# Convolution on raw padded rows: the second normalization moved from the data into the tap weights, and the last image split into quarters

## The chip, the core and the metric

One core of a Trainium2 chip runs the whole kernel. The metric is the device time of one execution in microseconds. Three runs of the kernel before took 4033.33, 4034.28 and 4036.42 us; the median is 4034.28.

Five engines work on their own queues, in the order in which the program issues to each: PE (TensorE, with its weight loads PEld), DVE (VectorE), ACT (ScalarE), POOL (GpSimd) and SP (SyncE, which here only issues DMAs).

## The reference, cut to what matters

The input x has 16 images of 56 x 56 positions with 384 channels, in float32. Both layers add a residual to a group normalization over 32 groups of 12 channels.

```
x = x + L0_conv(gn(x))      # window attention: 7x7 windows of the image rolled by 3, 12 heads of 32,
                            # w_qkv (1152x384), w_out (384x384), b_out, relative position bias and masks
x = x + L1_conv(gn(x))      # depthwise 3x3 convolution, zero padding, one sign (+1, 0, -1) per tap and channel
```

`gn(v) = (v - mean) / sqrt(var + 1e-5)`, per image and group of channels. With a scale a and a shift s per channel and image it is a*v + s. The zero padding stands around the normalized image, so that at the image's border fewer than nine taps see the shift s.

## The kernel before, in words

Channels lie on the 128 partitions, in NC = 3 blocks. An image is NS = 8 strips of 7 rows (a row of windows), a strip is two units of 4 windows; so there are NU = 16 units per image and 256 units, numbered u = 0 to 255. `all_units` (L1014) issues them one by one. The heavy work of a unit is on PE: `value`, `query_key` and `project` (three matmuls of 392 columns per output block), `scores` of the next unit, `add_up` and `attend` of this one. DVE adds the bias to the scores (`softmax`, L587, the operation e), takes part in the reciprocal (`invert`, L681 and L682), scales (`divide`, L689), turns values (`turn`, L527), and adds the residual (`project`, L708) with statistics (L714). ACT empties PSUM, takes exponentials (L605) and logarithms (L679, L680). `by_key` (L534) moves the turned values with 16 DMAs on SP, for which `add_up` of the next strip waits. PSUM has four banks for products (`bank`) and four for scores.

Beside this runs light work, at due times: `at(when, f, ...)` puts a function into the list of the unit int(when), at the fraction after the point. `plan_load` (L964) brings in the next image: `fetch_halves` issues on POOL (L450) the input DMAs of a strip two strips ahead, 12 for a strip of whole rows and 48 for the strip that wraps around the rolled image, which is the last of the eight. `plan_conv` (L946) does the second layer of the image before. `norm_gather` and `norm_scale` bring the statistics to POOL by DMA and compute a and s there; `center` (L731) derives the middle tap's coefficients. Then come six chunks, half an image (28 rows) and one channel block each, `step` units apart (2.6, for the last but one image 1.95), after a lead of 3 units:

- `band` (L742), SP: loads 30 rows of the strip sums, which `project` had written to the DRAM tile `mid`, into `xb`, of which there is one.
- `pad` (L777), ACT, L792: writes a*x + s into one of two zero-bordered tiles `hp`.
- `middle` (L808), ACT, L822: starts the sum `o` with the residual and the middle tap.
- `tap` (L824), DVE, L828: eight operations o = hp * w + o over 1568 elements.
- `turn_sum` (L832), DVE, L835, and `store` (L837), SP: turns the sum to tokens and writes it in eight DMAs.

The last image has no next one to hide behind. `plan_last` (L908) puts its statistics (`norm_products` with matmuls, L340), four chunks of the first two channel blocks on DVE, and the third channel block in four quarters on PE after the last unit: `convolve` (L849) adds 8 taps and the middle as nine matmuls for each of 28 pieces of 112 tokens (L865, L872), `carry` (L874) and `turn_late` (L888) write out. The bands are loaded in two parts, since the last strip, which holds the rows 52 to 55 and 0 to 2, is complete only at the end. At the very end a check value is computed (L1102 to L1111) and read by all engines; a second, safer program is skipped.

Of the kernel before, what the change touches and what calls it, by code (L numbers as in the profile page):

```python
# [34 lines left out]
def kernel(  # L35
# [30 lines left out]
    R = W + SHIFT  # L66
    LT = 2 * W
# [17 lines left out]
    bpool = ctx.enter_context(tc.tile_pool(name="xb", bufs=1))  # L85
# [23 lines left out]
    dw_t = const.tile([P, NC, 9], F32, tag="dw", name="dw_t")  # L109
    bias = const.tile([P, 2, NH, 2, T], F32, tag="bias", name="bias")  # L110
# [13 lines left out]
    hps = [const.tile([P, BR + 2, W + 2], F32, tag=f"hp{n}", name=f"hp{n}") for n in range(2)]  # L124

    accs = [const.tile([P, 2 * BR, D], F32, tag=f"o{n}", name=f"o{n}") for n in range(2)]
# [22 lines left out]
    def clear_conv():  # L149
        for t in (*xls, *hps, *accs):  # L150
            nc.gpsimd.memset(t, 0.0)
# [42 lines left out]
    def load_depthwise():  # L194
# [10 lines left out]
        nc.vector.tensor_copy(dw_t, pw[:, : NC * 9].rearrange("p (c t) -> p c t", c=NC))  # L205

    loaded_bias = []

    def load_bias(queue, first_q, last_q, fast):


        if not loaded_bias:
            rel = ypool.tile([P, NC, WIN, R], F32, tag="y", name="rel").rearrange("q c h w -> q (c h w)")[:, : T * NH]
            nc.gpsimd.memset(rel, 0.0)
            loaded_bias.append(rel)
# [15 lines left out]
        mask = ypool.tile([P, NC, WIN, R], F32, tag="y", name="mask").rearrange("q c h w -> q (c h w)")[:, : 2 * T]  # L231
# [80 lines left out]
    def fetch_late():  # L312
# [3 lines left out]
        def place(name, rows, width, at=None):  # L316
# [7 lines left out]
        hp = [  # L324
            place("hp_late", LR + 2, W + 2, xls[1].rearrange("p t c -> p (t c)")),
            place("hp_late2", LR + 2, W + 2),
        ]
        acc = [
            place("acc_late", LR, W + 2, xt.rearrange("p c k d -> p (c k d)")),
            place("acc_late2", LR, W + 2),  # L330
        ]
        for t in (*hp, *acc):
            nc.gpsimd.memset(t, 0.0)
        late_tiles.update(gm=gm, dg=dg, hp=hp, acc=acc)
# [5 lines left out]
    def norm_products(key, gm, meanwhile=()):  # L340
        st = stats.pop(key)
# [24 lines left out]
        for f, n in meanwhile[:1]:  # L366
            f(n)
# [7 lines left out]
        for f, n in meanwhile[1:]:  # L375
            f(n)
# [10 lines left out]
    def late_norm(b):  # L387
        norm_products((1, b), late_tiles["gm"])

    xs = {}  # L390
# [5 lines left out]
    def fetch(s):  # L396
        b, r = divmod(s, NS)
        xl = staging(s)
        first = r * WIN + SHIFT
# [38 lines left out]
    def fetch_halves(s, c):  # L438
# [6 lines left out]
        first = r * WIN + SHIFT  # L445
# [133 lines left out]
    def softmax(u, fast):  # L579
# [4 lines left out]
        if fast:  # L584
# [6 lines left out]
            bias[:, int(s % NS == NS - 1)].rearrange("q (i j) w k -> q i (j w) k", i=HPC),  # L591
# [99 lines left out]
    def project(s, m):  # L691
# [4 lines left out]
        if m == 0:  # L696
            ys[s] = ypool.tile([P, NC, WIN, R], F32, tag="y", name=f"y_{s}")
# [9 lines left out]
        view = ys[s][:, m, :, SHIFT:R]  # L707
# [7 lines left out]
        if m == NC - 1:  # L715
            if b not in mids:
                mids[b] = dram.tile([P, NC, H, R], F32, tag="mid", name=f"mid_{b}")
            del xs[s]
            yt = ys.pop(s)
            nc.gpsimd.tensor_copy(yt[:, :, :, 0:SHIFT], yt[:, :, :, W:R])  # L720
            r0 = r * WIN + SHIFT
            n = min(WIN, H - r0)
            queue = nc.sync if s == B * NS - 1 else nc.gpsimd
            queue.dma_start(mids[b][:, :, r0 : r0 + n, :], yt[:, :, 0:n, :])
            if n < WIN:
                queue.dma_start(mids[b][:, :, 0 : WIN - n, :], yt[:, :, n:WIN, :])
# [4 lines left out]
    def center(b, pool=nc.gpsimd):  # L731

        coef = coefs[1, b]
        cen = small.tile([P, NC, 2], F32, tag="cen", name=f"cen_{b}")
        pool.tensor_tensor(cen[:, :, 0], coef[:, :, 0], bo_sb, ALU.mult)
        pool.tensor_tensor(coef[:, :, 1], coef[:, :, 1], cen[:, :, 0], ALU.add)
        pool.tensor_tensor(cen, coef, dw_t[:, :, 4].unsqueeze(2).to_broadcast([P, NC, 2]), ALU.mult)
        pool.tensor_scalar(cen[:, :, 0], cen[:, :, 0], 1.0, None, ALU.add)
        pool.tensor_tensor(cen[:, :, 1], cen[:, :, 1], bo_sb, ALU.add)
        centers[b] = cen  # L740

    def band(b, k, c):  # L742
# [3 lines left out]
        xb = bpool.tile([P, BR + 2, R], F32, tag="xb", name=f"xb_{b}_{k}_{c}")  # L746
        nc.sync.dma_start(xb[:, at : at + hi - lo, :], mids[b][:, c, lo:hi, :])
        bands[b, k, c] = (xb, at, hi - lo)

    last_strip = ((0, (NS * WIN + SHIFT) % H), ((NS - 1) * WIN + SHIFT, H))  # L750

    def band_late(b, k, c, part):

        rows = LR if c == NC - 1 else BR
        lo, hi = max(k * rows - 1, 0), min((k + 1) * rows + 1, H)
        first = k * rows - 1
        if part == 0:
            size = (rows + 2) * R
            if c == NC - 1:
                xb = xpool.tile([P, NC, ST], F32, tag="x", name=f"xb_late_{k}").rearrange("p c n -> p (c n)")  # L760
            elif (k, c) == (0, 1):
                xb = qk.rearrange("p m n -> p (m n)")
            elif (k, c) == (1, 0):
                xb = bias.rearrange("p v h w n -> p (v h w n)")
            else:
                xb = bpool.tile([P, BR + 2, R], F32, tag="xb", name=f"xb_{b}_{k}_{c}").rearrange("p h w -> p (h w)")
            bands[b, k, c] = (xb[:, :size].rearrange("p (h w) -> p h w", w=R), lo - first, hi - lo)
        xb = bands[b, k, c][0]
        parts = [(last_strip[0][1], last_strip[1][0])] if part == 0 else last_strip
        for p0, p1 in parts:  # L770
            p0, p1 = max(p0, lo), min(p1, hi)
            if p0 < p1:
                nc.sync.dma_start(xb[:, p0 - first : p1 - first, :], mids[b][:, c, p0:p1, :])

    count, padded = [0], {}

    def pad(b, k, c, late=False):  # L777

        coef = coefs[1, b]
        xb, at, n = bands.pop((b, k, c))  # L780
        rows = LR if late else BR
        if late:
            hp = late_tiles["hp"][k % 2]
        else:
            hp = hps[count[0] % 2]
            outs[b, k, c] = accs[count[0] % 2]
            count[0] += 1
        if k == 0:
            nc.gpsimd.memset(hp[:, 0, :], 0.0)
        if k == H // rows - 1:  # L790
            nc.gpsimd.memset(hp[:, rows + 1, :], 0.0)
        nc.scalar.activation(  # L792
            hp[:, at : at + n, 1 : W + 1],
            xb[:, at : at + n, 0:W],
            AF.Identity,
            bias=coef[:, c, 1:2],
            scale=coef[:, c, 0:1],
        )
        padded[b, k, c] = (hp, xb)
# [8 lines left out]
    def middle(b, k, c, late=False, first=False):  # L808

        xb = padded[b, k, c][1]  # L810
        cen = centers[b][:, c]
        if late:
            acc = late_tiles["acc"][k % 2]
            outs[b, k, c] = acc
            to, rows = acc[:, :, :W], xb[:, 1 : LR + 1, 0:W]
        else:
            to, rows = sum_of(b, k, c), by_half(xb[:, 1 : BR + 1, 0:W])
# [244 lines left out]
    with tc.manual_schedule():  # L1062
# [11 lines left out]
        for n, home in ((0, hps[1]), (1, accs[0])):  # L1074
            fetch_weights(n, home)
# [100 lines left out]
```

## Time and profile before

| What | us |
|---|---|
| median of the three runs | 4034.28 |
| the profiled execution's own time | 4037.27 |
| its span | 4035.5 |
| PE busy | 3951.8 (98%) |
| DVE busy | 3493.2 (87%) |
| ACT busy | 2227.1 (55%) |
| POOL busy | 1867.7 (46%) |
| taps, L828, 752 operations on DVE | 1378.1, 1833 ns each |
| last softmax addition (unit 255) | starts at 3925.15 |
| last output DMA issued | 4028.60 |

The own time is the whole execution, and the span runs from the first to the last instruction. Busy time is summed per engine; engines overlap. A line of a group has the line in the code, the engine, the operation, what it writes and reads, its shape and its count, then the busy time and the mean of one in ns, then the engine's idle time ahead of it and what ended most of it. In a line in order of time the start comes first and then the duration, both in us. Starts of two operations of one engine that follow each other are a little closer than a duration, since an operation overlaps the next.

### The profile page before, as it was taken

How to read it: one execution, taken by the hardware profiler on the slowest of the kernel's cores; microseconds unless marked ns; L12 is line 12 of the kernel's file. 1: busy time of each engine (PE TensorE's matmuls, PEld its weight loads, DVE VectorE, ACT ScalarE, POOL GpSimd, SP SyncE). 2: the span in 40 equal slices, each digit the busy share in tenths (PEclk: the TensorE clock that was granted, in tenths of full speed). 3: DMA queues.
4: the chain of work that ended last, by engine and by line, in shares of the span. 5: the costliest groups of instructions: out<-in, count | busy, mean ns of one | idle time of the engine just before them, and what ended most of it. 6: DMA issues, size and time to landing. Idle time of an engine off the chain costs nothing.

```text
span 4035.5 us, 144674 instructions
## 1 busy us (share of the span) xinstructions
PE 3951.8 (98%) x63189; PEld 2415.2 (60%) x63189; DVE 3493.2 (87%) x3718; ACT 2227.1 (55%) x4690; POOL 1867.7 (46%) x3159
## 2 busy tenths in 40 slices
PE   7999999999999999999999999999999999999987
PEld 5665655655656565655656556555555656556657
DVE  4546989899898998989899898988989899898897
ACT  3545556556564656556556565656556556564542
POOL 5454545455453564545455453554545355452000
PEclk9999999999999999999999999999999999999998
DMA  4323545454554554545454554554545454543444
GB/s 108 82 68 88 113 111 116 107 123 104 113 119 102 124 114 103 114 112 117 109 122 111 111 114 103 128 109 103 112 113 116 107 122 111 112 114 81 113 108 100
DMA packets 802162, 439.36 MB, mean 109 GB/s; under 512 B 671478, under 2 KB 752023, under 8 KB 801518
## 3 DMA queue, kind: packets, MB, share of 16 engines
q1 hardware_dynamic: 711110, 268.40, 30.5%
q0 software_dynamic: 87648, 159.12, 16.7%
q8 instruction: 498, 8.16, 0.9%
q10 hardware_dynamic: 2760, 2.48, 0.2%
q14 instruction: 146, 1.20, 0.1%
HBM read 170.08 MB, written 158.45 MB: 81 GB/s over the span
## 4 chain that ended last, share of the span: by engine, by line
PE 29%; issue 23%; POOL 21%; DVE 13%; DMA 10%; ACT 1%; SPq 1%; DVEq 0%; POOLq 0%; ACTq 0%
POOL xl L450 14%; PE pq L503 11%; PE pv L516 6%; PE py L700 6%; DVE o L828 6%; DMA mvd<-mv 2%; DMA xl<-in_x_dram 2%; PE score_banks L570 2%; PE po L661 2%; DVE xt L467 2%; DVE e L587 1%; POOL dev L287 1%; PE score_banks L640 1%; DMA cod<-both 1%; DMA gt<-mvd 1%
## 5 line engine op out<-in xcount | busy, mean ns | idle before, releaser
L503 PE MATMUL pq<-xn,wq_t 128*128 128x392 f32 x4608 | 1584.9, 496 | 0.0
L450 POOL DMA_DIRECT2D xl<-in_x_dram x1980 | 1329.3, 727 | 144.0 <-DVE xt L467 96.5
L828 DVE SCALAR_TENSOR_TENSOR o<-hp,dw_t,o 128x1568 f32<-128x1568 f32 x752 | 1378.1, 1833 | 5.4
L503 PEld LDWEIGHTS pq<-xn,wq_t 128*128 128x128 f32 x4608 | 845.4, 188 | 595.4 <-ACT x L482 0.2
L516 PE MATMUL pv<-xn,wq_t 128*128 128x392 f32 x2304 | 815.5, 497 | 13.6 <-DVE y L708 13.6
L700 PE MATMUL py<-ot,wo_t 128*128 128x392 f32 x2304 | 818.1, 500 | 7.9 <-DVE ot L689 7.0
L510 ACT COPY qk<-pq 128x392 f32<-128x392 f32 x768 | 367.3, 482 | 566.9 <-PE pq L503 566.4
L720 POOL COPY y<-y 128x63 f32<-128x63 f32 x128 | 62.7, 490 | 1240.3 <-DVE y L708 1240.3
L700 PEld LDWEIGHTS py<-ot,wo_t 128*128 128x128 f32 x2304 | 425.1, 190 | 311.7 <-DVE ot L689 25.9
L516 PEld LDWEIGHTS pv<-xn,wq_t 128*128 128x128 f32 x2304 | 424.3, 189 | 312.9 <-DVE y L708 15.6
L605 ACT ACTIVATE e<-e 128x1176 f32<-128x1176 f32 x256 | 303.3, 1185 | 497.8 <-DVE e L587 496.8
L681 DVE SCALAR_TENSOR_TENSOR ln<-score_banks,inv 128x588 f32<-128x588 f32 x256 | 195.8, 765 | 323.6 <-ACT inv L680 323.1
L523 ACT COPY vt<-pv 128x392 f32<-128x392 f32 x384 | 188.7, 491 | 369.9 <-PE pv L516 369.0
L570 PEld LDWEIGHTS score_banks<-qk 32*49 32x49 f32 x24576 | 266.0, 117 | 145.1 <-issue 114.6
L587 DVE SCALAR_TENSOR_TENSOR e<-score_banks,bias 128x1176 f32<-128x1176 f32 x256 | 347.0, 1356 | 5.9 <-PE score_banks L570 5.9
L661 PEld LDWEIGHTS po<-e,v 49*32 49x32 f32 x24576 | 311.5, 105 | 51.7 <-issue 2.6
L479 ACT COPY x<-xt 128x196 f32<-128x196 f32 x720 | 225.5, 367 | 175.5 <-DVE xt L467 175.4
L661 PE MATMUL po<-e,v 49*32 49x49 f32 x24576 | 309.3, 212 | 1.6 <-issue 1.6
L570 PE MATMUL score_banks<-qk 32*49 32x49 f32 x24576 | 298.2, 218 | 2.9 <-DVE ln L681 2.9
L527 DVE STREAM_TRANSPOSE vq<-vt 128x512 f32<-128x512 f32 x384 | 265.6, 693 | 8.4 <-ACT vt L523 5.3
L708 DVE TENSOR_TENSOR y<-py,x 128x392 f32<-128x392 f32 x384 | 213.1, 555 | 42.5 <-PE py L700 42.3
L492 ACT ACTIVATE xn<-x,coef 128x392 f32<-128x392 f32 x384 | 247.0, 711 | 4.4 <-DVE coef L381 4.4
(177 smaller groups left out, 3301.9 us busy)
## 6 DMA issues: line engine op xcount, KB each, us to landing
v<-vq SPq DMA_DIRECT2D x2048, 48.0 KB
xb<-mid SPq DMA_DIRECT2D x90, 855.5 KB
out_dram<-o SPq DMA_DIRECT2D x736, 98.0 KB
mid<-y POOLq DMA_DIRECT2D x112, 619.5 KB
xl<-in_x_dram POOLq DMA_DIRECT2D x1260, 52.5 KB
mid<-y POOLq DMA_DIRECT2D x15, 354.0 KB
xl<-in_x_dram POOLq DMA_DIRECT2D x180, 28.0 KB
mid<-y POOLq DMA_DIRECT2D x15, 265.5 KB
```

The costliest lines, as they stand in the source:

```text
L450: nc.gpsimd.dma_start(xz[i * D + lo : i * D + hi, c, k : k + n, :], flat[token : token + n * (hi - lo)].rearrange("(k t) c -> t k c", k=n) ...
L492: nc.scalar.activation(xn[:, c, :, :T], xs[s][:, c, :].rearrange("p (w t) -> p w t", t=T), AF.Identity, bias=coef[:, c, 1:2], scale=coef[: ...
L503: nc.tensor.matmul(pq[:, :ST].rearrange("p (w t) -> p w t", t=T), wq_t[:, c, m * P : (m + 1) * P], xn[:, c, :, :T], start=(c == 0), stop=( ...
L510: nc.scalar.copy(qk[:, m, :ST], pq[:, :ST])
L516: nc.tensor.matmul(pv[:, :ST].rearrange("p (w t) -> p w t", t=T), wq_t[:, c, 2 * C + m * P : 2 * C + (m + 1) * P], xn[:, c, :, :T], start= ...
L527: nc.vector.transpose(vq[:, :, :, m].rearrange("p h n d -> p n h d"), vt[:, m].rearrange("p (n w) (j b) -> p n (w j) b", w=2, b=D),)
L570: nc.tensor.matmul(pp[row * HT : row * HT + rows, i, k0 : k0 + T], qk[part, NC * fast + j, q0 : q0 + rows], qk[part, NC * (not fast) + j, ...
L587: nc.vector.scalar_tensor_tensor(e, pp[:, :, : NC * 2 * T].rearrange("q i (n k) -> q i n k", k=T), QSCALE, bias[:, int(s % NS == NS - 1)]. ...
L605: nc.scalar.activation(flat, flat, AF.Exp, accum_out=reach[:, 0, u : u + 1])
L661: nc.tensor.matmul(po[w][i * D : (i + 1) * D, (2 * j + r) * T : (2 * j + r + 1) * T], vs[s][keys, i, n * 2 + r, j], by_head(u)[keys, i * N ...
L700: nc.tensor.matmul(py[:, :ST], wo_t[:, c, m * P : (m + 1) * P], ots[s][:, c, :], start=(c == 0), stop=(c == NC - 1),)
L828: nc.vector.scalar_tensor_tensor(acc, by_half(hp[:, dy : dy + BR, dx : dx + W]), dw_t[:, c, t : t + 1], acc, ALU.mult, ALU.add)
```

## The change

The convolution no longer reads normalized rows. `project` writes its sums into rows of PW = 60 columns with a zero column on each side of the 56, and `band` loads these raw rows, with a zero row at the image's top or bottom. The normalization's scale goes into the weights: `center` computes 9 scaled tap weights per channel for each image (`aw`). The shift cannot go into one constant, because the taps that fall on the padding see none of it; so `center` computes nine constants per channel, one for each region (inside, left, right, top, bottom and corners), from sums of taps (`edge`, computed once). `begin` starts the sum with the residual, the middle tap and the region's constant: one activation for the whole chunk, then five over the border columns, the border row and its two corners. `pad`, `middle` and the two `hp` tiles are gone; there are two `xb` and three `o`.

The strips of an image are taken in another order: the wrapping one is now the first (`first_row`), so that the last strip holds the rows 45 to 51. For the last but one image the step is 1.8 units and the lead 2.7.

The last image is split into quarters of 14 rows. Its taps are taken with the unscaled weights and on raw rows, and a separate step multiplies by the scale and adds the rest when the coefficients are there (`late_finish`, and `late_join` for the third block). So taps of the first two quarters are issued in the last 2.6 units on DVE, and 17 matmuls of the third block on PE; `convolve` now multiplies a diagonal matrix with 392 columns of rows, one matmul per tap without the middle. The last strip reaches its band by a copy on ACT (`late_rows`), not through DRAM. `late_out` turns each quarter with transposes and writes it.

```diff
+    def first_row(s):
+        return (s % NS - 1) % NS * WIN + SHIFT
...
+            nc.gpsimd.memset(yt[:, :, :, 0 : W + 2 : W + 1], 0.0)
+            if s == B * NS - 1:
+                late_tiles["rows"] = yt
+                return
...
+        pool.tensor_tensor(cen[:, :, :9], edge, coef[:, :, 1].unsqueeze(2).to_broadcast([P, NC, 9]), ALU.mult)
+        pool.tensor_tensor(cen[:, :, :9], cen[:, :, :9], bo_sb.unsqueeze(2).to_broadcast([P, NC, 9]), ALU.add)
+        pool.tensor_tensor(cen[:, :, 9], coef[:, :, 0], dw_t[:, :, 4], ALU.mult)
+        pool.tensor_scalar(cen[:, :, 9], cen[:, :, 9], 1.0, None, ALU.add)
+        if b < B - 1:
+            aw = small.tile([P, NC, 9], F32, tag="aw", name=f"aw_{b}")
+            pool.tensor_tensor(aw, dw_t, coef[:, :, 0].unsqueeze(2).to_broadcast([P, NC, 9]), ALU.mult)
...
-        nc.scalar.activation(
-            hp[:, at : at + n, 1 : W + 1],
-            xb[:, at : at + n, 0:W],
-            AF.Identity,
-            bias=coef[:, c, 1:2],
-            scale=coef[:, c, 0:1],
-        )
...
+        affine(b, c, sum_of(b, k, c), by_half(xb), 0)
+        for n, x in ((1, 0), (2, W - 1)):
+            affine(b, c, acc[:, :, x and end], xb[:, :, x], n)
+        row = k and BR - 1
+        affine(b, c, sum_of(b, k, c)[:, row], by_half(xb)[:, row], 6 if k else 3)
+        for n, x in ((1, 0), (2, W - 1)):
+            at = x and end
+            affine(b, c, acc[:, row, at : at + 1], xb[:, row, x : x + 1], (6 if k else 3) + n)
...
-            acc, by_half(hp[:, dy : dy + BR, dx : dx + W]), dw_t[:, c, t : t + 1], acc, ALU.mult, ALU.add
+            acc, by_half(xb[:, dy : dy + BR, dx : dx + W]), scaled[b][:, c, t : t + 1], acc, ALU.mult, ALU.add
...
+    def late_tap(q, c, t):
+        dy, dx = divmod(t, 3)
+        acc, xb = late_sums[q, c], late_bands[q, c]
+        nc.vector.scalar_tensor_tensor(
+            acc, xb[:, dy : dy + QR, dx : dx + W], dw_t[:, c, t : t + 1], acc, ALU.mult, ALU.add
+        )
...
+            nc.tensor.matmul(
+                late_banks[q, half][:, :ST].rearrange("p (h w) -> p h w", w=W),
+                late_tiles["dg"][:, t],
+                late_bands[q, NC - 1][:, row : row + WIN, dx : dx + W],
...
+        starts = (-2.6, -1.9, -1.15, -0.6)
+        for (q, c), when, wide in zip(pieces, starts, (0.7, 0.7, 0.5, 0.2)):
+            when += first
+            at(when - 1.2, late_band, q, c)
+            at(when - 0.15, late_begin, q, c)
+            for i, t in enumerate(some):
+                at(when + wide * i / 7, late_tap, q, c, t)
...
+        at(first - 1.7, convolve, 4)
+        at(first - 1.3, convolve, 9)
+        at(first - 0.9, convolve, 4)
...
+        next_(norm_products, (1, B - 1), late_tiles, ((convolve, 2), (taps, 2, 0, (1, 2, 3))))
+        next_(center, B - 1, nc.vector)
+        next_(convolve, 9)
+        for q in range(2):
+            for c in range(2):
+                next_(late_middle, q, c)
+        next_(taps, 2, 0, (5, 6, 7, 8))
+        next_(late_middle, 0, joined)
+        next_(late_middle, last, 0)
+        for q in range(2):
+            for c in range(2):
+                next_(late_finish, q, c)
+                next_(late_out, q, c)
+        next_(late_join, 0)
+        next_(late_out, 0, joined)
+        next_(convolve, 10)
...
+        next_(convolve, 16)
+        next_(late_middle, 2, 1)
+        next_(late_middle, last, joined)
+        next_(taps, last, 0, some)
+        next_(late_finish, 2, 1)
+        next_(late_out, 2, 1)
+        next_(late_middle, 2, joined)
+        next_(late_finish, last, 0)
+        next_(late_out, last, 0)
+        next_(late_join, 2)
...
-            at(when - 0.35 * step, pad, p, k, c)
-            at(when - 0.25 * step, middle, p, k, c)
+            at(when - 0.3 * step, begin, p, k, c)
...
-            plan_conv(b - 1, NU * b, 2.6 if b < B - 1 else 1.95, 3, 0.4, nc.gpsimd)
+            last = b == B - 1
+            plan_conv(b - 1, NU * b, 1.8 if last else 2.6, 2.7 if last else 3, 0.4, nc.gpsimd)
```

## The prediction

> **What bounds it now.** I read the page's busy shares first, then a table of stages, then the last 110 us in order of time. In the page's first part TensorE is busy for 98% of the span, and the stage table says where the rest lies. Its columns are: the stretch and its length in us, then the busy us (with instructions) of PE, PEld, DVE, ACT and POOL, the granted clock, the DMA share and GB/s.
>
> ```profile
> 3540.00:3780.00 240.00, 239.60 (x3902) 144.39 (x3902) 212.70 (x220) 134.32 (x265) 83.13 (x144) 1.00 0.44 100
> 3780.00:3930.00 150.00, 140.59 (x2513) 85.72 (x2514) 142.44 (x129) 76.80 (x143) 8.53 (x18) 0.97 0.46 106
> 3930.00:4036.00 106.00, 79.49 (x606) 74.58 (x591) 76.00 (x69) 26.73 (x32) 2.80 (x9) 0.81 0.45 108
> ```
>
> The reader is to see three regimes. Up to 3780 PE never rests at clock 1.00: no step beside it can gain anything. From 3780 to 3930 DVE is at 95%: the last 10 units are nearly DVE's. After 3930 there is a tail of 106 us in which nothing is full. So the change can win in the tail alone, and pays wherever it puts DVE work ahead of it.
>
> The tail, DVE in order of time (start, us, engine and line, operation; in brackets its idle time before):
>
> ```profile
> 3925.15 1.38 DVE L587 SCALAR_TENSOR_TENSOR e<-score_banks,bias 128x1176 f32<-128x1176 f32 x1
> ...
> 3930.83 0.77 DVE L681 SCALAR_TENSOR_TENSOR ln<-score_banks,inv 128x588 f32<-128x588 f32 x1 [2.35 <-ACT inv L680]
> 3931.63 0.77 DVE L682 SCALAR_TENSOR_TENSOR ln<-ln,inv 128x588 f32<-128x588 f32 x1
> 3932.50 0.77 DVE L689 TENSOR_TENSOR ot<-ot,ln 128x588 f32<-128x588 f32 x1
> 3937.63 0.57 DVE L708 TENSOR_TENSOR y<-py,x 128x392 f32<-128x392 f32 x1 [4.36 <-PE py L700]
> ```
>
> The first line is the last softmax addition, that of unit 255; I measure everything from it. The last output DMA is issued at 4026.72 + 1.88 = 4028.60, that is 103.45 us later, and 6.9 us after it the span ends. Within these 103.45: statistics complete 18.4 us after the anchor, coefficients at 27.7 (3952.84), then four chunks of taps on DVE and 28 groups of nine matmuls on PE.
>
> **The order in images 1 to 14** (a listing of both programs by engine): DVE has the same operations in the same places, PE the same. ACT loses the padding copy L792 (1.76 us) and the centre L822 (1.71), next to each other 3.26 a chunk, and gains one full activation and five small ones. The small ones, 1 to 56 elements with a scale and a bias, have no row. From 784 elements (1.036 us) and 1568 (1.706) a fixed part of 0.37 follows, 0.28 to 0.30 when they overlap as L338's do; the 21-element copy L482 (0.21, some 0.12 overlapped) is the lower end. I take 0.29, since the rows with scale and bias are nearer: 1.61 + 5 x 0.29 + 0.2 for waits on itself = 3.3. No change, on an engine that is half idle. POOL gets a 42-element memset in front of each mid write, a row memset for each band, and in the norm chain three operations more (0.2 to 0.5 each); the first activation needs the last but one of them, 1.3 us later, and is itself 0.13 of a unit (2 us) later than the padding was. The 48 small input DMAs of the wrapping strip (27.7 us of POOL) move from the eighth to the thirteenth unit of an image. There POOL stood idle for 11.4 us and 20.05 us ahead of two y copies and for 6.0 ahead of the statistics' DMA, against 20.8 us more to issue: hidden, and worth up to a few us of delay in the norm chain if that idle time is gone. Each band's DMA on SP, and POOL's row memset, now wait for the last tap (DVE) of the chunk two before, not for ACT's reading of the last. Behind it on SP stand the 16 v moves, for which the next even unit's add_up waits; behind it on POOL the input DMAs. DVE stands there at the same place in the program, at most 3 us late: nothing to 0.1 us a chunk. At the start DVE gets six reductions of some 0.17 (as L1106), where it waits 13.1 us for ACT's copies: 0 to 1. Sum of these stages: 0, from -5 (PE's two rests of 1.0 and 0.3 us per image, a quarter of them gone) to +18 (below).
>
> **Units 240 to 255.** The anchor moves. Starts give 1.80 us per tap in this stage, 1.93 for a turned chunk, 1.28 for e, 2.36 for the three of ln/ot, 1.08 for y and its statistics, 0.63 for vq. A late tap of 784 elements has no row; from 588 (0.77) and 1568 (1.835) it is 0.98, 1.0 in a chain, 0.95 at best. From e of unit 245 to e of unit 255 DVE now does 41 taps and 5 turns, after the change 40 taps, 5 turns and 10 late taps: -1.8 + 9.7 = +8. By units it is 16.2, 14.4, 16.2, 14.4, 16.2, 14.4, 16.3, 14.3, 16.4, 13.4 = 152.2, against 147.5 measured now (same pitches: 144.5). A unit of PE is 15.0, so the backlog has nowhere to go: at least 4.7 late, 8 if the waits that exist now stay. I take 6.5. In front of it, the first chunk starts 0.16 unit earlier (2.4 us), its coefficients 1.3 later, and ACT already waited 2.37 for them in this image: vt and qk copies, queued behind, then PE, lose 0 to 3; I take 1.5. Anchor: +8 (5 to 11). PE's 17 early matmuls of 0.675 (24 records took 8.10 for 12) fill units in which PE rested.
>
> **The tail, from the anchor.** DVE: e and 7 late taps 8.3, ln to ot 2.36, 8 late taps, y, 3 late taps, y, y: 24.9 (now 17.5: its waits for PE are filled, and more). Statistics to coefficients as now 9.2, and wider constants: 36. Then three engines are tied. ACT does six regional sets, each one large activation (702 or 756 elements, 0.87 or 0.91 when overlapped) and small ones, four with five (2.32), two with two (1.49): 12.3, to 48, before its first copy out; PE's transposes have two of four banks (two hold sums), and wait. Four outputs, PE and ACT in turn, 7 transposes 1.55 each: 6.2, copy 0.5: 55. Ten matmuls 6.75: 61.7; two outputs 3.1: 64.8; sixteen matmuls 10.8: 75.6; an output and its copy 2: 77.6; ACT's set 1.5, the join 1.1: 80; DVE's seven taps 7.0 and join 1.1: 88; two outputs 3.1, copies 0.9, issue 0.8: 93. DVE has 69 us of work in it and waits some 10 for that join, behind sixteen matmuls.
>
> PE rests some 6 us before 48 and 2.5 before the last outputs. What that costs:
>
> ```profile
> 3955.30:3957.30 2.00, 2.00 (x9) 2.00 (x10) 1.97 (x2) 2.00 (x2) 0.00 (x0) 0.50 0.02 4
> 3957.30:3959.30 2.00, 2.00 (x12) 2.00 (x11) 1.96 (x2) 2.00 (x2) 0.00 (x0) 0.50 0.00 0
> 3959.30:3961.30 2.00, 2.00 (x11) 2.00 (x11) 1.97 (x2) 1.10 (x2) 0.00 (x0) 0.50 0.00 0
> 3961.30:3963.30 2.00, 2.00 (x20) 2.00 (x19) 1.96 (x2) 0.00 (x0) 0.00 (x0) 0.99 0.00 0
> ```
>
> After 4.7 us of rest the granted clock is 0.50 for 5.9 us, so 3 us of work are lost (again at 3989, after 3.29 us of rest). The Trainium skill (TensorE: Matmul & The Clock Gate, Part 1: The HAM clock gate) has one busy window of about 3.4 us release the clock: 1.7 lost, and speaks against this order, which lets PE rest while ACT works. By the rule 2 rests are 3.4, by the row 6; the second rest is short and may cost nothing. I take 4.5: 97.5 against 103.45, so -6 (-10 to -2 with small activations of 0.12 and clock losses of 0 to 6).
>
> **Sum.** Anchor +8, tail -6, images 0: +2 us. The profiled execution is 4037.27 (span 4035.5 and 1.8 around it), 3.0 above the median of the runs; its sum gives 4039.3, and the median 4034.28 + 2 = 4036.3. A measurement of this kernel tells 0.2% (8 us) from no change, so 4026.2 and 4042.3 are the bounds.
>
> **Rivals.** (1) Faster: DVE's extra taps fill only time that is idle now (anchor +4.7), PE never cools, small activations cost 0.12: 4.7 + 89.5 - 103.45 = -9, and PE's rests of 1.3 us per image go in one image of four (-5): 4020. For it: 68 us of taps and turns now lie after 3953, and some 37 are all that DVE keeps after its coefficients. Against it: PE and ACT do not get shorter with DVE. (2) Slower: the six activations in one block, where two stood apart, hold ACT's ln, exp and qk copies. Place: each of 90 chunks. Now padding and centre delay ln at 2091.18, ot comes late, and PE rests 0.29 us, at one chunk of six. With 0.2 at each: +18, 4054. It decides from 0.07 us a chunk, which with the +2 reaches 0.2%. Against it: PE has four banks, and ACT is at 57%. (3) It does not do what it says: bands on SP, queued behind stores that wait for turns, land late, and the 28 early taps stand still on DVE, which holds e and y up: +10, 4046. Against it: the first band is queued 1.05 units (16 us) ahead of its first reader.
>
> **Chances.** As summed 0.42 (4027 to 4042), (1) 0.30, (2) 0.20, (3) 0.08. So faster by over 0.2% 0.30, within 0.42, slower 0.28. The range takes the middles of (1) and (2) in: 4016 to 4054; the likeliest case's own is 4027 to 4042.
>
> **What would show it.** Right: e of unit 255 some 8 us later; y's without waits for PE; coefficients 36 us after the anchor; PE idle some 6 us while ACT does sets, then clock 0.50; a DVE wait of about 10 us for ACT ahead of a join. Wrong: DVE idle between units 245 and 255, ACT or PE waits per image other than 1.3 us, late taps off 1.0, or a join that waits for nothing. What would make the forecast wrong most easily is a small steady gain or loss: 0.5 us per image is as much as everything in the tail.

## The result, and the profile after

The changed kernel takes 4049.96 us (median of six runs, 4049.18 to 4051.72). Runs of the kernel before that alternated with it have a median of 4035.53, and the ratio is 1.0037 (95% interval 1.0026 to 1.0048): 14.4 us slower. The profiled execution took 4051.72, the slowest of the six, with a span of 4049.9. I cut the two traces at three points that both have, the softmax addition e on DVE of units 0, 240 and 255:

| Stretch of the profiled span, us | before | after | difference |
|---|---|---|---|
| start, up to e of unit 0 | 74.72 | 78.98 | +4.3 |
| images, e of unit 0 to e of unit 240 | 3627.1 | 3643.4 | +16.3 |
| last units, e of unit 240 to e of unit 255 | 223.34 | 231.72 | +8.4 |
| tail, e of unit 255 to the end of the span | 110.35 | 95.78 | -14.6 |
| span | 4035.5 | 4049.9 | +14.4 |

The same stages as in the table of before (stretch, length, busy us of PE, PEld, DVE, ACT, POOL, granted clock, DMA share, GB/s):

```profile
3540.00:3780.00 240.00, 237.35 (x3803) 142.06 (x3802) 214.30 (x222) 132.64 (x295) 74.22 (x133) 1.00 0.44 104
3780.00:3930.00 150.00, 147.09 (x2429) 87.62 (x2428) 145.41 (x132) 80.91 (x163) 6.58 (x22) 1.00 0.47 109
3930.00:4050.00 120.00, 90.06 (x706) 55.20 (x704) 93.86 (x122) 52.16 (x111) 2.77 (x9) 0.86 0.36 99
```

The first row matters: PE had 239.60 of 240 us before and has 237.35 now. A stage in which PE never rested has got rests. The tail on DVE, against the lines shown of before:

```profile
3954.12 1.38 DVE L586 SCALAR_TENSOR_TENSOR e<-score_banks,bias 128x1176 f32<-128x1176 f32 x1
3955.41 7.32 DVE L859 SCALAR_TENSOR_TENSOR o<-xb_late,dw_t,o 128x784 f32<-128x784 f32 x7
3962.66 0.76 DVE L680 SCALAR_TENSOR_TENSOR ln<-score_banks,inv 128x588 f32<-128x588 f32 x1
...
3965.01 8.40 DVE L859 SCALAR_TENSOR_TENSOR o<-xb_late,dw_t,o 128x784 f32<-128x784 f32 x8
3973.33 0.56 DVE L707 TENSOR_TENSOR y<-py,x 128x392 f32<-128x392 f32 x1
```

The waits of 2.35 us ahead of ln and 4.36 ahead of y are gone, filled with late taps, but y comes 19.2 us after e and not 12.5 as before.

**Where an image loses.** With e listed unit by unit, the lag grows at two places of each image: by 0.34 us at the seventh unit and by some 0.95 at the ninth (0.85 to 1.06 from the fifth image on). The rest is one step of 0.86 in the first image, a few of 0.2 to 0.4, and 1.75 us that came back in units 202 and 203. ACT between e of unit 103 and e of unit 104, before and then after:

```profile
1640.68 1.76 ACT L792 ACTIVATE hp<-xb,coef 128x1624 f32<-128x1624 f32 x1
1642.34 0.48 ACT L510 COPY qk<-pq 128x392 f32<-128x392 f32 x1
1644.58 0.63 ACT L479 COPY x<-xt 128x196 f32<-128x196 f32 x2 [1.75 <-DVE xt L467]
1645.24 0.21 ACT L482 COPY x<-xt 128x21 f32<-128x21 f32 x1
1645.54 1.70 ACT L822 ACTIVATE o<-xb,cen 128x1568 f32<-128x1568 f32 x1
```

```profile
1652.91 0.48 ACT L509 COPY qk<-pq 128x392 f32<-128x392 f32 x1 [1.49 <-PE pq L502]
1653.29 3.70 ACT L789 ACTIVATE o<-xb,cen 128x1568 f32<-128x1568 f32 x6
1656.89 0.61 ACT L478 COPY x<-xt 128x196 f32<-128x196 f32 x2
1657.53 0.21 ACT L481 COPY x<-xt 128x21 f32<-128x21 f32 x1
```

Before, the padding stood ahead of the x copies, ended in time, and ACT even waited 1.75 us for DVE; the centre came behind them. Now one block of 3.70 us stands ahead of them. The next view is DVE behind it:

```profile
1657.78 0.57 DVE L482 BATCH_NORM_STATS2 st<-x 128x6 f32<-128x392 f32 x1 [0.86 <-ACT x L481]
1658.26 0.55 DVE L707 TENSOR_TENSOR y<-py,x 128x392 f32<-128x392 f32 x1
1658.85 0.57 DVE L713 BATCH_NORM_STATS2 st<-y 128x6 f32<-128x392 f32 x1
1659.33 1.37 DVE L586 SCALAR_TENSOR_TENSOR e<-score_banks,bias 128x1176 f32<-128x1176 f32 x1
```

DVE waits 0.86 us for the x copy, e is issued behind it, and DVE has no slack in the next 20 us to catch up (it worked without a pause from 1658.26 to 1678.1). So ot is late, and PE, an engine away from the cause and 26 us later, stops 0.75 us for it:

```profile
1683.92 2.24 PE L699 MATMUL py<-ot,wo_t 128*128 128x392 f32 x6 [0.75 <-DVE ot L688]
```

At the seventh unit it is the same block at 1614.10, ahead of two qk copies; there PE waits 0.40 us for ACT's qk directly. At the other four chunks of an image the lag doesn't grow.

### The profile page after: what moved, and what is told of

It reads as the page before. It is cut to its first block, busy times and chain, and to the rows that moved or that the text cites. A ratio compares the mean times of both kernels' runs of the same rounds, so it can differ in the third digit from the quotient of the medians.

```text
span 4049.9 us, 144668 instructions
## 1 busy us (share of the span) xinstructions
PE 3950.4 (98%) x62869; PEld 2381.5 (59%) x62869; DVE 3497.7 (86%) x3760; ACT 2257.1 (56%) x5111; POOL 1901.8 (47%) x3312
## 3 DMA queue, kind: packets, MB, share of 16 engines
q1 hardware_dynamic: 701662, 269.19, 29.5%
## 4 chain that ended last, share of the span: by engine, by line
PE 45%; DVE 17%; ACT 5%; DMA 5%; POOL 5%; issue 5%; SPq 1%; DVEq 0%; ACTq 0%; POOLq 0%
PE pq L502 17%; PE py L699 10%; PE pv L515 9%; DVE o L795 5%; PE score_banks L569 4%; PE po L660 2%; DVE e L586 2%; PE score_banks L639 2%; DMA xl<-in_x_dram 2%; ACT o L789 2%; POOL dev L295 2%; DVE y L707 1%; DVE st L713 1%; POOL xl L449 1%; DMA mvd<-mv 1%
## 5 line engine op out<-in xcount | busy, mean ns | idle before, releaser
L795 DVE SCALAR_TENSOR_TENSOR o<-xb,aw,o 128x1568 f32<-128x1568 f32 x720 | 1319.2, 1832 | 4.3
L719 POOL COPY y<-y 128x63 f32<-128x63 f32 x128 | 38.6, 302 | 801.3 <-DVE y L707 801.3
L789 ACT ACTIVATE o<-xb,cen 128x1568 f32<-128x1568 f32 (+1 forms) x540 | 323.2, 630 | 14.1 <-POOL cen L742 4.8
L482 DVE BATCH_NORM_STATS2 st<-x 128x6 f32<-128x392 f32 x360 | 198.9, 556 | 63.5 <-ACT x L481 63.3
```

Of the source, the lines that this page charges most:

```text
L789: nc.scalar.activation(to, of, AF.Identity, bias=cen[:, n : n + 1], scale=cen[:, 9:10])
L795: nc.vector.scalar_tensor_tensor(acc, by_half(xb[:, dy : dy + BR, dx : dx + W]), scaled[b][:, c, t : t + 1], acc, ALU.mult, ALU.add)
```

## The experiments

The theory: the six activations of `begin` as one block on ACT cost the steady 1.29 us per image, the start is late because of the strips' order, and the last units and the tail are DVE's and PE's sums. Rivals: ACT's total and not the place; the strips (POOL); the faster step. All ratios are against runs of the kernel before that alternated with the experiment. The table at the end of this section has the stretches of all.

**e1_split: the same work in two places**

```diff
-            at(when - 0.3 * step, begin, p, k, c)
+            at(when - 0.35 * step, start_sum, p, k, c)
+            at(when - 0.25 * step, borders, p, k, c)
```

> Change: in images 0 to 14 the six activations of a chunk are issued in two places, the full one where the padding stood and the five of the border where the centre stood (0.35 and 0.25 of a step ahead of the chunk); the same work. Theory: the loss of 1.29 us per image (0.34 at its seventh unit, 0.95 at its ninth) comes from the six standing in one block of 3.7 us on ACT, ahead of the copies of x and of qk. Then it is gone, unit 200 starts its softmax some 5 us after the kernel before (now 19.6), and the total is 4034 to 4036. Rival A: it is the longer total of the six (3.70 against 1.75 + 1.71 = 3.46) that ACT cannot place; then most of the loss stays: 4047 to 4050. Rival B: it isn't ACT at all but the other order of the strips (small DMAs on POOL) : 4050.

Measured: 4034.5 us, ratio 0.9994 (0.9986 to 1.0003). From unit 0 to 240 it takes 3629.3 us, 14.1 less than the changed kernel, with the same instructions. So the block is the cause of the loss; the strips on POOL (rival B) are out. Of PE's waits from 1120 to 3440 us (total, times, longest) the one for qk is gone, and the one for ot has shrunk (the changed kernel's lines stand at e6):

```profile
PE py L699 <- DVE ot L688: 4.9, 11, 0.6
```

**e2_no_borders: the five left out**

```diff
-            at(when - 0.3 * step, begin, p, k, c)
+            at(when - 0.3 * step, start_sum, p, k, c)
```

> Change: in images 0 to 14 the five border activations of a chunk are left out (border rows and columns get the constant of the inside), the full one stays where it is. Theory (block on ACT) and rival A (total on ACT) both give no steady loss, since ACT has 1.7 us in one place: 4033 to 4036. Rival B (strips, POOL): 4050, unchanged.

Measured: 4020.51, ratio 0.9962 (0.9948 to 0.9975). I had expected 4033 to 4036, since I had thought that before had no loss on ACT. It has: its padding and centre hold ot up at one chunk of an image, as rival (2) of the prediction had read at 2091.18. With 1.7 us per chunk on ACT the images take 3618.6, that is 8.5 less than before. So rival A is partly right: a second loss, of some 0.6 us per image, goes with what stands on ACT and was in the kernel before, too.

**e6_borders_pool: the five on POOL**

```diff
+            at(when - 0.35 * step, start_sum, p, k, c)
+            at(when - 0.33 * step, borders, p, k, c)
...
-        nc.scalar.activation(to, of, AF.Identity, bias=cen[:, n : n + 1], scale=cen[:, 9:10])
+        nc.gpsimd.tensor_scalar(to, of, cen[:, 9:10], cen[:, n : n + 1], ALU.mult, ALU.add)
```

> Change: in images 0 to 14 the full activation of a chunk stands on ACT where the padding stood, and the five border operations are done by POOL (same operands) just behind it. Theory: the kernel without borders took 4020.5, 14 us less than with the six split in two places (4034.5), so ACT's total per chunk is worth some 1.0 us per image more than its place; POOL, busy 47%, has room for 450 small operations of 0.2 to 0.5 us: 4020 to 4024. Rival A: POOL works in order, and its waits for DVE (801 us ahead of the y copies) and for input DMAs stand in front of the borders, so that taps on DVE wait: 4035 or more. Rival B: the 14 us were the time of the taps waiting for the borders' data, not ACT: as split, 4034.

Measured: 4023.18, ratio 0.9968 (0.9956 to 0.998), with all of the computation. The images take 3618.5. The waits of PE from 1120 to 3440 us, first of before, then of the changed kernel, then of this one (total, times, longest):

```profile
PE pv L516 <- DVE y L708: 9.2, 9, 1.1
PE py L700 <- DVE ot L689: 2.8, 10, 0.4
```

```profile
PE pv L515 <- DVE y L707: 9.0, 9, 1.1
PE py L699 <- DVE ot L688: 7.2, 10, 1.0
PE pq L502 <- ACT qk L509: 4.0, 10, 0.6
```

```profile
PE pv L515 <- DVE y L707: 8.8, 9, 1.1
```

The rest for y stays in all three. The waits for ot and qk are the ones that follow ACT's placing: 2.8 us before, 11.2 after, none here. From unit 70 to unit 222 the changed kernel loses 11.0 us against before; these waits are 8.4 of them, and the rest stands in no wait of the list. POOL's waits cost nothing: it does an operation of the border in 0.61 to 0.66 us, in gaps that it had.

**e7_spread: the five one by one on ACT**

```diff
+            at(when - 0.35 * step, start_sum, p, k, c)
+            for part in range(5):
+                at(when - (0.31 - 0.04 * part) * step, borders, p, k, c, part)
```

> Change: in images 0 to 14 the full activation stands where the padding stood, and the five border activations one by one, 0.04 of a step (1.6 us) apart, from 0.31 to 0.15 of a step ahead of the chunk; ACT's work is the same. Theory: it is the length of what stands in front of a waiting copy that counts, and pieces of 0.4 us delay a copy by 0.4 at most: 4024 to 4030, nearer to the kernel without borders than the split one. Rival: it is the sum on ACT: 4034 as the split one.

Measured: 4025.71, ratio 0.9974 (0.9965 to 0.9984). The images take 3618.0, as without the borders, and of PE's wait for ot one is left:

```profile
PE py L699 <- DVE ot L688: 0.4, 1, 0.4
```

So it isn't ACT's total: in the images of these profiles the same six activations cost 25 us in one block, 11 in two pieces and nothing in six. The totals say a little less. This profile fell on the fastest of ten runs, and that of e1 on the slowest of thirteen; by the medians the block stands 24.3 us above the six pieces and the two pieces 8.8, and the six pieces themselves stand 5.2 above e2. Where these 5.2 lie is not shown.

Nor is it the longest piece alone. The full activation is still one piece of 1.72 us, at 0.35 of a step here and at 0.3 in e2, and costs nothing in the images; before, with no piece over 1.76, loses 9 us there. What before and e1 have is a second long piece, at 0.25 of a step, and both fall behind e7 at the seventh unit of an image (by 0.8 and 1.0 us, of which 0.35 comes back at the ninth). So what counts is how much stands in one piece in front of a due copy. That it is the second piece that costs before its 9 us follows from these places; no run takes it away there.

**e8_first_image_old_order and b1_before_again: the start**

```diff
-        return (s % NS - 1) % NS * WIN + SHIFT
+        return (s % NS - (s >= NS)) % NS * WIN + SHIFT
...
-            bias[:, int(s % NS == 0)]
+            bias[:, int(first_row(s) + WIN > H)]
```

> Change: the strips of the first image alone are taken in the order of before (the wrapping one last). Theory: the 1.5 to 5.4 us by which the first softmax starts late in the five profiles of the changed kernel come from the first strip's input, which is now the wrapping one, with more and smaller input DMAs ahead of all others: then the first softmax starts within 1 us of 74.7 and the total falls by 3 to 4 us: 4046. Rival: it is chance in the loads of a start or the other places of the weights: the first softmax at 76 to 80 as now, the total unchanged at 4050.

> The kernel before, once more, for the spread of its start: theory (the start is slower by the change): first softmax at 74.7, within 0.5 us; rival (chance): anywhere from 74 to 80.

Measured: 4048.29, ratio 1.0031 (1.002 to 1.0043); and 4035.44 for the kernel before, ratio 0.9999 (0.9989 to 1.0009). The first e starts at 75.70 and 75.95. Over all profiles it is 74.7 to 76.4 in the five with the old order and 76.2 to 80.7 in the nine with the new, 75.7 against 78.9 in the mean: 3.2 us, with a spread of its own, so neither theory is right alone. The late start begins with ACT's first copy of the input (20.95 us, before 17.46), behind the loads of the image. The total fell by only 1.7 us, and the two intervals overlap; the start is shown in the traces, not in the totals.

**e4_join_early: the third join's constant earlier**

```diff
         next_(late_middle, 2, 1)
+        next_(late_middle, 2, joined)
         next_(late_middle, last, joined)
...
-        next_(late_middle, 2, joined)
         next_(late_finish, last, 0)
```

> Change: in the tail the three activations that give the third join its constant are issued 6 + 2 activations and copies earlier, ahead of the copies of an output. Theory: the wait of 5.05 us of DVE ahead of that join is for those three, which stand on ACT behind copies that wait for PE's sixteen matmuls; the join's matmuls are done about 4 us earlier. Then the wait shrinks to under 1 us, the seven taps behind it start 4 to 5 us earlier and the total is 4045 to 4046. Rival: PE's sums are the late side too (the seven transposes and the last matmuls are behind it): the wait stays at 3 or more, 4048 to 4050.

Measured: 4048.17, ratio 1.0029 (1.002 to 1.0037). The join on DVE, in the changed kernel and then here:

```profile
4029.09 1.16 DVE L914 SCALAR_TENSOR_TENSOR xb_late<-score_banks,coef,xb_late 128x392 f32<-128x392 f32 x2 [5.05 <-ACT xb_late L789]
```

```profile
4025.12 1.16 DVE L914 SCALAR_TENSOR_TENSOR xb_late<-score_banks,coef,xb_late 128x392 f32<-128x392 f32 x2
```

The wait is gone, and the tail is 92.04 us instead of 95.78. In the totals 1.8 us are seen, not the 4 to 5 expected, and the two intervals overlap; the start, which varies by more, may hide the rest.

**e5_taps_later: seven taps behind the statistics**

```diff
+                if (q, c) != (1, 1):
                     at(when + wide * i / 7, late_tap, q, c, t)
...
-        next_(norm_products, (1, B - 1), late_tiles, ((convolve, 2), (taps, 2, 0, (1, 2, 3))))
+        next_(norm_products, (1, B - 1), late_tiles, ((convolve, 2), (taps, 1, 1, (1, 2, 3))))
         next_(center, B - 1, nc.vector)
+        next_(taps, 1, 1, (5, 6, 7, 8))
...
+        next_(taps, 2, 0, some)
         next_(late_middle, 2, 0)
```

> Change: the seven late taps of the fourth early piece (second quarter, second block) are issued after the last statistics instead of in the last unit, three of them inside the wait for the group means, and the seven taps of the third quarter's first block move behind the first join. The same work. Theory: the last unit's residual additions wait on DVE behind these taps (PE waits 4.57 us for one of them), so the statistics and the coefficients come 7 us earlier, and the taps fall into 10 us of DVE's waits further on: 4044 to 4046. Rival: DVE is what ends the tail, and seven taps later are seven taps later: 4049 to 4051.

Measured: 4050.68, ratio 1.0034 (1.0021 to 1.0046): nothing. The first half came true: PE's wait for y is gone, and the last constant is ready 29.5 us after e of unit 255, not 35.2. It was given back: the taps moved behind the first join hold an output up, whose transposes stand on PE ahead of sixteen matmuls. PE is idle 3.64 us, the matmuls end 71.8 us after e of unit 255 (72.0 in the changed kernel), and the third join waits 7.89 us:

```profile
4008.16 3.21 PE L942 MATMUL px<-ident,xb_late 128*116 128x128 f32 x14 [3.64 <-issue]
```

```profile
4026.28 1.16 DVE L914 SCALAR_TENSOR_TENSOR xb_late<-score_banks,coef,xb_late 128x392 f32<-128x392 f32 x2 [7.89 <-ACT xb_late L789]
```

**e3_old_step and e12_no_early_taps: the last units**

```diff
-            plan_conv(b - 1, NU * b, 1.8 if last else 2.6, 2.7 if last else 3, 0.4, nc.gpsimd)
+            plan_conv(b - 1, NU * b, 1.95 if last else 2.6, 3, 0.4, nc.gpsimd)
```

> Change: the convolution of the last image but one at a step of 1.95 units after a lead of 3, as before, instead of 1.8 after 2.7. Theory: the 8.4 us that units 240 to 255 lose are DVE's sum of work up to the last softmax (ten late taps more), which the step doesn't change: units 243 to 252 come up to 3 us earlier, unit 255 within 1.5 us of now, the total 4048 to 4051. Rival: it is the faster step that loses them: unit 255 comes 5 us or more earlier and the total is 4045 or less.

Measured: 4055.72, ratio 1.005 (1.0036 to 1.0063). Up to unit 253 nothing at all is lost against before, and then 9.7 us in the last two units: 233.00 us for the stretch, within 1.3 of the changed kernel, as a sum of DVE's work would have it. So the faster step only spreads the loss over earlier units. The total is higher than I expected, by 5.8 us over the changed kernel; the profile, which fell on the fastest of five runs, shows 2.3 of these (start +1.7, images -1.8, last units +1.3, tail +1.1), and the rest stays unexplained.

```diff
             for i, t in enumerate(some):
-                at(when + wide * i / 7, late_tap, q, c, t)
+                if (q, c) == (1, 1):
+                    at(when + wide * i / 7, late_tap, q, c, t)
```

> Change: the 21 taps of the first three early pieces are left out (those outputs lack seven of nine taps). Ten of them stood ahead of the last softmax and eleven behind it. Theory: DVE is full there, so each counts with 0.96 us: the last softmax comes 8 to 10 us earlier (units 240 to 255 lose 0 or less), and behind it PE no longer waits 4.6 us for the residual addition, 7 to 9 us more: 4032 to 4035. Rival: DVE had room for them in its waits, and the loss came from the step or the bands' DMAs: under 5 us: 4045 or more.

Measured: 4043.13, ratio 1.002 (1.0011 to 1.0029); the last units take 226.26 us, the tail 91.95. DVE now waits in two places that the taps had filled:

```profile
3949.35 1.38 DVE L586 SCALAR_TENSOR_TENSOR e<-score_banks,bias 128x1176 f32<-128x1176 f32 x1 [1.69 <-PE score_banks L569]
...
3957.85 0.77 DVE L680 SCALAR_TENSOR_TENSOR ln<-score_banks,inv 128x588 f32<-128x588 f32 x1 [7.12 <-ACT inv L679]
```

So the theory is half wrong: the ten taps ahead of e cost 5.5 of the 8.4 us, not 9.6, and the eleven behind it 3.8. The other 2.9 us of the last units are not theirs. PE's seventeen early matmuls (11.5 us) are the next suspect, since DVE waits for PE's scores here, but no run took them away: that stays open.

**e9_combined and e10_tail_order: together**

e9 has the changes of e6, e4 and e8. e10 has those of e6, e8 and e5, and this order in the tail (its core):

```diff
+        next_(late_join, 1)
+        next_(late_middle, last, 1)
+        next_(late_out, 2, 0)
+        next_(late_out, 1, joined)
+        next_(convolve, 12)
...
+        next_(late_middle, 2, joined)
+        next_(late_out, 2, 1)
...
+        next_(late_join, 2)
+        next_(convolve, 6)
+        next_(late_out, last, 0)
+        next_(late_out, 2, joined)
+        next_(convolve, 12)
```

> Three of the changes above together: borders on POOL, the third join's constants earlier, the first image in the old order of strips. Theory (the three losses lie in different places and add): 4023.2 - 3.8 - 2.5 = 4017. Rival: the join's gain depends on when the output DMAs on SP are done, and those at the end are one chain: only 1.8 of it, as in the totals: 4019 to 4020.

> Change against the combined one: seven taps of the fourth early piece after the statistics, as in the kernel with taps later, and PE's matmuls of the third and fourth quarter (12, 6 and 12) no longer behind outputs that wait for those taps; the third join's constant right behind its matmuls. Theory: with taps later the coefficients came 7.3 us earlier but PE's sixteen matmuls ended at the same time, because they were queued behind the transposes of an output that waited for DVE; with that order mended the end comes 3 to 5 us earlier than in the combined one: 4012 to 4014. Rival: ACT and the output DMAs on SP take over: 4016 to 4018.

Measured: 4015.11, ratio 0.9949 (0.9935 to 0.9962), and 4013.28, ratio 0.9943 (0.9929 to 0.9956). The gains of e9 add up (4017 was expected), and both versions beat both kernels, by some 20 and 35 us, with all of the computation. e10's order gains nothing that can be told from e9, though its forecast, 4012 to 4014, was met: its tail is 91.08 us against 90.93. DVE's last output operation ends 79.1 us after e of unit 255 instead of 80.4, but the last two outputs then come to the end together, and behind a rest of PE, so that their transposes run at clock 0.50:

```profile
3999.44 3.21 PE L956 MATMUL px<-ident,wq_t 128*116 128x128 f32 x14 [4.57 <-issue]
```

In e9 the last seven take 0.98 us.

| Stretch, us | start | images | last units | tail | span |
|---|---|---|---|---|---|
| before | 74.72 | 3627.1 | 223.34 | 110.35 | 4035.5 |
| after | 78.98 | 3643.4 | 231.72 | 95.78 | 4049.9 |
| e1_split | 80.15 | 3629.3 | 229.29 | 97.37 | 4036.1 |
| e2_no_borders | 77.20 | 3618.6 | 228.12 | 94.70 | 4018.6 |
| e6_borders_pool | 78.17 | 3618.5 | 228.13 | 96.99 | 4021.8 |
| e7_spread | 78.76 | 3618.0 | 229.06 | 94.63 | 4020.5 |
| e8_first_image_old_order | 75.70 | 3644.0 | 230.55 | 96.87 | 4047.1 |
| b1_before_again | 75.95 | 3625.2 | 223.53 | 108.96 | 4033.6 |
| e4_join_early | 80.01 | 3643.6 | 231.66 | 92.04 | 4047.3 |
| e5_taps_later | 76.21 | 3643.5 | 231.80 | 96.30 | 4047.8 |
| e3_old_step | 80.71 | 3641.6 | 233.00 | 96.92 | 4052.2 |
| e12_no_early_taps | 79.44 | 3643.7 | 226.26 | 91.95 | 4041.3 |
| e9_combined | 76.38 | 3617.8 | 228.01 | 90.93 | 4013.1 |
| e10_tail_order | 75.72 | 3617.3 | 228.29 | 91.08 | 4012.4 |

## Why the prediction was right or wrong, point by point

The likeliest case (no change, 4036.3) was wrong; 4049.96 is the side of rival (2), whose chance was put at 0.20. It lies inside the stated range, 4016 to 4054, because that range took in the middle of rival (2), and outside the likeliest case's own, 4027 to 4042. That it comes so near to rival (2)'s 4054 is in part luck: the start cost 4.3 us where 0 to 1 was put, and the tail gave 14.6 where 6 was.

**Images 1 to 14: wrong, and the step that failed.** It said of ACT's new activations: "No change, on an engine that is half idle". A share of 55% says nothing of the moment. The step costed the sum of six activations and not what is queued behind the last of them. Where it put 0, the runs show two terms: some 9 us that before lost came back (e7), and the block cost 25. Rival (2) had the mechanism and nearly the price: 0.2 us at each of 90 chunks, measured 1.29 per image of six chunks (0.215 a chunk), but at two chunks of the six, and through the x copies as well as qk. The term itself was mis-sized too: 3.3 us of ACT's time per block, measured 3.60 from its start at 1653.29 to that of the next operation at 1656.89. The groups of the changed kernel:

```profile
L789 ACT ACTIVATE o<-xb,cen 128x1568 f32<-128x1568 f32 x90 | 155.1, 1723 | 5.0 <-POOL cen L742 4.8
L789 ACT ACTIVATE o<-xb,cen 128x28 f32<-128x28 f32 x180 | 69.2, 433 | 3.0
L789 ACT ACTIVATE o<-xb,cen 128x1 f32<-128x1 f32 x180 | 59.9, 380 | 3.0
L789 ACT ACTIVATE o<-xb,cen 128x56 f32<-128x56 f32 x90 | 39.0, 433 | 3.0
```

The durations are near those of the Trainium skill (ScalarE: Activation LUTs, What ACT_TABLE_LOAD costs): an estimate from its figures, with scale and bias as pointers, is 0.37 us for one element and 0.40 for 28, measured 0.38 and 0.43. Its overlap of 0.093 between neighbours holds at two of the five boundaries in the block. The 180 operations on columns (28 elements) sum to 77.9 us of durations and are busy for 69.2, so the two of a block overlap by 0.097; the two on corners (one element) overlap by 0.094. At the other three boundaries ACT rests instead: 3.0 us in each of the last three groups, 0.033 for each of 90 blocks. At these three the operation writes elements that the one just before it has written; the two columns, and the two corners, are apart. Against an overlap such a boundary costs 0.13 us, three of them 0.39, where the forecast had 0.2 for "waits on itself"; the rest is the longer column and row operations. In e7_spread the next operation of ACT starts 0.28 to 0.34 behind a small one, as the 0.29 had it.

**POOL and SP in the images: right.** The wrapping strip's DMAs, the memsets and the norm chain cost nothing that can be seen: e7_spread has them all, and its images are 9 us faster than before.

**The start, 0 to 1: wrong.** It looked at six reductions on DVE and not at the order of the first loads: +4.3 in this profile, 3.2 in the mean of all.

**Units 240 to 255, +8: right in size (+8.4), in part for another reason.** Its sum by units held when the step was changed (e3: 9.7 against 8.4). But the late taps are 5.5 us of it, not 9.7, so that the size is in part luck, since DVE had waits for ACT and PE there that the sum took for full.

**The tail, -6: right in its path, wrong in two terms.** Its marks, from e of unit 255, against the trace: coefficients and constants at 36, measured 35.2; first copy out at 48, measured 47.7; ten matmuls done at 61.7, measured 59.5; sixteen at 75.6, measured 72.0; last join at 88, measured 84.6; last issue at 97.5, measured 88.5. Two terms failed, because they count one half clock twice. Seven transposes were put at 1.55 us. They take about that at clock 0.50: the four outputs from 4000.23 on take 6.72 us, where the sum had 6.2. At full clock seven take 0.93 to 0.98, and the trace of before had shown that rate with 14 in 1.69 us. First the line of before, then two of the changed kernel:

```profile
4021.63 1.69 PE L898 MATMUL px<-ident,o 128*128 128x128 f32 x14
```

```profile
4000.23 1.75 PE L942 MATMUL px<-ident,xb_late 128*116 128x128 f32 x7 [4.72 <-DVE xb_late L914]
4002.39 4.56 PE L942 MATMUL px<-ident,xb_late 128*116 128x128 f32 x21 [0.41 <-ACT e L943]
```

The 4.5 us of clock loss, added on top, are half of the 9.0 by which the last issue came early; the rest is outputs at full clock, and transposes that begin 46.1 us after e, ahead of ACT's first copy out. How long the half clock lasts, in windows of the changed kernel:

```profile
3999.80:4003.22 3.42, 2.58 (x11) 2.18 (x12) 3.35 (x5) 3.42 (x10) 0.00 (x0) 0.50 0.00 0
4003.22:4006.63 3.41, 3.41 (x18) 3.41 (x17) 3.30 (x4) 2.55 (x6) 0.00 (x0) 0.50 0.81 208
...
4030.52:4033.94 3.42, 3.42 (x9) 2.16 (x8) 3.31 (x4) 1.06 (x2) 0.00 (x0) 0.50 0.72 181
```

PE starts again at 4000.23 after a rest of 4.72 us, and the clock (sixth figure behind the stretch) is 0.50 until 4006.63: 6.4 us; before, with the restart at 3955.29 and the change at 3961.34, it was 6.05 (the forecast had 5.9). The forecast had taken the Trainium skill's busy window of about 3.4 us for the whole delay. The same section (TensorE: Matmul & The Clock Gate, Part 1: The HAM clock gate) says that this window runs free and doesn't start with the work, and the trace agrees. Its stretches at one clock begin and end 3.41 us or a multiple of it apart (0.50 from 3996.39 to 4006.63 and from 4030.52 to 4033.94, 1.00 between), and the rows are cut at these places. Both times the half clock ends with the first row that PE fills; the row that it fills for 2.58 us doesn't end it. So a restart takes what is left of one window and then a whole one: up to 6.8 us at half clock, an estimate from the page's figure. The wait ahead of the third join was forecast at 10 us for ACT, and is 5.05.

**Rivals.** (1) named a real gain, but of the two rests of PE per image it is the smaller one, for ot, that can go, and in every image; the one for y stays in all versions. With it e6's images are 8.6 us shorter than before's, and the block hid this. (3), late bands, was wrong: no wait of DVE for a band stands among the long ones between 3700 and 3956 us.

## What to carry to other kernels

An engine's busy share doesn't say what a block of work on it costs: look for the first copy queued behind the block, who waits for it, and whether that engine has slack to catch up. Cut work that isn't urgent into pieces and place them one by one between the urgent ones; the same six instructions cost some 25 us in one piece and little or nothing in six. When a wait is taken away in a chain of in-order queues, follow the moved work to its new place first, and see which engine has something queued behind it.

## What the runs showed of the hardware

- An operation of 1 to 56 elements with scale and offset from a tile took 0.38 to 0.44 us on ACT, and 0.61 to 0.66 on POOL, in the mean of each size.
- Two such operations in a row on ACT overlapped by 0.094 to 0.097 us when they wrote different elements, and had a gap of 0.033 when the second wrote elements of the first (90 blocks of the changed kernel).
- Seven transposes of 128 x 116 took 0.93 to 0.98 us at clock 1.00, where nothing held them up, and 1.70 to 1.75 at 0.50.
- After a rest of PE of 4.7 us the clock was 0.50 for 6.05 us (before) and 6.4 (after) from PE's restart, until the end of the first window of 3.41 us that PE filled.
- The first loads vary: ACT's first copy of the input started at 18.8 to 21.8 us in the nine profiles with the wrapping strip first, and at 17.4 to 18.6 in the five with the old order, so kernels with the same start differ by up to 3.0 us.
